# Moving four pieces of another stream's VectorE work inside a hand-ordered LSTM stage

## The chip, the cores and the metric

The kernel runs on one core of a Trainium2 chip. The metric is the device time of one execution in microseconds (us); each figure for a kernel is the median of several executions. The core has a matrix engine (TensorE, PE in the profile), a vector engine (VectorE, DVE), an activation engine (ScalarE, ACT), a general engine (GpSimd, POOL), and a sync engine (SyncE, SP) whose queue issues nearly all transfers here. Each engine takes its own instruction list, and semaphores tie the lists together.

## The reference

The input x is 128 graphs of 64 nodes with 256 channels, in f32. Four layers follow each other, each of the form x = x + layer(relu(layernorm(x))):

```
h = relu(layernorm(x)); x = x + gcn_with_batchnorm(h, adj, W1, W2)     # layer 0
h = relu(layernorm(x)); x = x + gcn_and_lstms(h, adj, Wg0, Wg1, ...)   # layer 1
h = relu(layernorm(x)); x = x + causal_attention(h, Wqkv, Wo)          # layer 2
h = relu(layernorm(x)); x = x + masked_attention(h, W, adj)            # layer 3
```

The change lies in layer 1. There h goes through two graph convolutions, relu(adj @ (h @ Wg)), and then through four LSTMs in a row. The LSTM number p (1 to 4) takes each graph's 64 nodes in windows of p nodes, runs p steps over a window from a zero state, and writes the last hidden state over the window's last node:

```
for p in 1..4:
    last = lstm(Wih[p-1], Whh[p-1], bias, windows of p nodes of h)
    h[:, p-1::p] = last
```

## The kernel before

The 8192 rows are cut into 16 chunks of 512 rows. Two chunks make a superchunk, so that layer 1 runs its LSTMs eight times, for superchunks 0 to 7. The LSTMs of one superchunk are a long chain of TensorE products and of gate work on the other engines. Between its links the kernel places work of other chunks by hand: the convolutions of the chunks of a later superchunk, and, for chunks whose LSTMs are done, the residual sum and the normalization that layer 2 needs. Nothing is scheduled by a planner: on TensorE, VectorE, ScalarE (from superchunk 0 on), GpSimd and SyncE, instructions are put into their queues in the order in which the program is written.

The program walks through the LSTMs with a generator, `lstms`, which yields at marked places. The marks have numbers: 0 to 3 in the one-token LSTM (`single`), 4 to 7 in the two-token one, 8 to 13 in the three-token one, 14 to 21 in the four-token one; a half (15.5, 19.5) is the place in the middle of a step. At each mark the loop runs the units that are listed for that number, one step of another generator each. The tuples that name the marks are the subject here:

- `CONV` and `FIRST` (the latter in superchunk 0) hold the marks for the next superchunk's two chunks in `convolutions`. `BEGUN` holds the marks for the first steps of the chunks after those. The first tuple of a pair is for the even chunk, the second for the odd one.
- The steps of `convolutions` are in order: scale (L900, two VectorE or ScalarE instructions into the tile `cv`); transpose (L988, two VectorE instructions into `ym`), after which SyncE writes `ym` to memory (L247), reads it back in another order into `cv` (L254) and loads the chunk's x into `xs` (L995); sum the two (`add_squares`, two instructions at L284); take the normalization's statistics (L159, L160, then two GpSimd instructions, L99 and L100); apply it in two halves (a small VectorE instruction L194, then two ScalarE instructions at L196 for each half); then products (`agg_b`, v, u, `agg_c`) and their evacuations.
- `AHEAD` and `FINAL` (the latter in superchunk 7) hold the marks of `ahead` for chunks whose layer 1 is done: write and reorder `xs`, statistics, two halves of the normalization, then `channel_squares` (four 32x32 block transposes by VectorE at L272, from `h` into `nm`), after which SyncE writes `nm` to memory for layer 2.

A step s of a p-token LSTM forms its gates from seven products each ("kinds") that share PSUM banks named x, y and z. VectorE adds a finished bank to the gates (L1164), and only then may TensorE put the next product into the same bank. ScalarE copies (L1161) and applies sigmoid and tanh (L1084); VectorE forms the cell (L1234, L1235) and the new state `hs` and its differences `hd` (L1093, L313 to L316), which the next step's products read. The first step of an LSTM is different: TensorE writes g (L1126), ScalarE applies the gate functions (L1113), VectorE forms the cell (L1119). At the end of superchunk's LSTMs VectorE forms the first operand sum `xd` of the next superchunk (L313), whose one-token LSTM starts with products at L1340, copies at L1360 and gate additions at L1364.

In superchunk 7 no convolutions are left, and short runs of transposes of an identity (`keep_busy`, L151) stand at some marks.

Of the kernel before, what the change touches and what calls it, by code (L numbers as in the profile page):

```python
# [19 lines left out]
def kernel(  # L20
# [1412 lines left out]
    def new_hT(sc):  # L1433

        hTs[sc] = l1r.tile([P, KD, SUP * CH], F32, tag="hT", name=f"hT_{sc}")
# [48 lines left out]

    RESIDUAL = (0, 3, 4), (2, 5, 5.5)
    CONV = (3, 4, 4, 5, 5.5, 7, 8, 9, 10, 10), (3, 4, 4, 11, 11.5, 13, 14, 15, 15.5, 17, 18, 20)
    BEGUN = (11, 11, 13, 14, 16), (17, 17.5, 19)
    FIRST = (1, 2, 3, 3, 4, 4, 5, 5.5, 7, 8, 9, 10, 10), (3, 3, 5.5, 7, 8, 8, 11, 11.5, 13, 14, 15, 15.5, 17, 18, 20)
    AHEAD = (4, 5, 7, 12, 14, 15), (6, 7)
    LATE = 5, 6, 8, 9  # L1490
    IDLE = {5: 4, 7: 18, 9: 10, 13: 14, 15: 8}
    FINAL = (4, 5, 10, 12, 12, 14), (6, 7, 11, 14, 14, 16)
    START = (0, 1, 0, 0, 0, 1, 0, 1, 1, 0, 0, 1, 1, 0, 1, 2, 2)

    tc.no_sync_barrier()
# [22 lines left out]
    with tc.manual_schedule(engines={mybir.EngineType.PE, mybir.EngineType.DVE, mybir.EngineType.Pool,  # L1518
                                     mybir.EngineType.Activation, mybir.EngineType.SP}):
        last = NCH // SUP - 1  # L1520
        for sc in range(last + 1):
            todo = {}

            def units(places, unit):
                for n in places:
                    todo.setdefault(n, []).append(unit)
# [4 lines left out]
            if sc < last:  # L1531
                for i in range(SUP):
                    units((CONV if sc else FIRST)[i], convs[(sc + 1) * SUP + i])
                new_hT(sc + 1)
# [7 lines left out]
            if sc:  # L1542
                for i in range(SUP):
                    units((FINAL if sc == last else AHEAD)[i], aheads[(sc - 1) * SUP + i])
            if sc + 1 < last:
                for i in range(SUP):
                    units(BEGUN[i], convs[(sc + 2) * SUP + i])
            n = -1
# [434 lines left out]
    def store(c, t):  # L1983
# [3 lines left out]
        for r in range(2):  # L1987
# [18 lines left out]

    FIRST = """table+0 load2+2 q2+0 copyq2+0 res1+14 res1+15 v2a+0 v2b+0 score2+0 res1+14 res1+15
               exp2+0 q2+1 divide2+0 copyq2+1 load2+3 turn2+0 v2a+1 v2b+1 out2+0 keep+0 res1+14 res1+15
# [10 lines left out]
    def run(order, c):  # L2019
        for name in order.split():  # L2020
            i = max(name.find("+"), name.find("-"))
            steps[name[:i]](c + int(name[i:]))

    with tc.manual_schedule(engines={mybir.EngineType.PE, mybir.EngineType.DVE,
                                     mybir.EngineType.Activation, mybir.EngineType.Pool,
                                     mybir.EngineType.SP}):
        run(FIRST, 0)
        close_l1r()
# [61 lines left out]
```

## Time and profile before

The time before is 1878.06 us, the median of 3 runs (1877.81 to 1878.57). The profiled execution spans 1877.4 us.

| what | profile before |
|---|---|
| TensorE busy | 1847.4 us, 98% |
| VectorE busy | 1245.6 us, 66% |
| ScalarE busy | 1014.0 us, 54% |
| GpSimd busy | 550.2 us, 29% |
| superchunks 0 to 7 of layer 1 | from about 276 us to 1506 us, 154.8 us each |
| sums, L284 of `convolutions`, one instruction | 0.69 us median |
| squares, L272, one instruction | 0.40 us median |
| statistics, L159, one instruction | 0.39 us median |
| VectorE's wait for the load of `xs` before L284 | 6.3 us in 6 times |

In a timeline, a line has the start, the time from the start to the end of the last instruction merged into it, the engine, the source line, the operation, the tiles (output<-input), the shape, the count, and in brackets the idle time of the engine before it and what ended it. Such times are from the start of the span. The end of a matmul is modelled, and matmuls overlap, so the step from one start to the next tells more of TensorE than its busy time: it is 0.11 us for 128 columns, 0.14 for 168, 0.22 for 256 and 0.43 for 512, and each f32 product is two MATMUL instructions.

### The profile page before, as it was taken

How to read it: one execution, taken by the hardware profiler on the slowest of the kernel's cores; microseconds unless marked ns; L12 is line 12 of the kernel's file. 1: busy time of each engine (PE TensorE's matmuls, PEld its weight loads, DVE VectorE, ACT ScalarE, POOL GpSimd, SP SyncE). 2: the span in 40 equal slices, each digit the busy share in tenths (PEclk: the TensorE clock that was granted, in tenths of full speed). 3: DMA queues.
4: the chain of work that ended last, by engine and by line, in shares of the span. 5: the costliest groups of instructions: out<-in, count | busy, mean ns of one | idle time of the engine just before them, and what ended most of it. 6: DMA issues, size and time to landing. Idle time of an engine off the chain costs nothing.

```text
span 1877.4 us, 39077 instructions
## 1 busy us (share of the span) xinstructions
PE 1847.4 (98%) x15077; PEld 1476.8 (79%) x15077; DVE 1245.6 (66%) x3150; ACT 1014.0 (54%) x2284; POOL 550.2 (29%) x704
## 2 busy tenths in 40 slices
PE   8999989999999999999999999999999999999998
PEld 6877856895897798699589689778968967777776
DVE  6768855566577666667666766666565567776776
ACT  5766635556456456555655645655565544444453
POOL 5855722122222212212322312222132114332232
PEclk9999999999999999999999999999999999999999
DMA  3223652134334433332433443343144254444433
GB/s 115 71 70 141 238 200 92 66 129 152 107 130 147 145 141 127 113 136 95 150 119 132 165 137 130 130 132 125 60 142 140 70 157 136 145 149 139 144 113 114
DMA packets 111273, 241.45 MB, mean 129 GB/s; under 512 B 11504, under 2 KB 74864, under 8 KB 111088
## 3 DMA queue, kind: packets, MB, share of 16 engines
q1 hardware_dynamic: 110192, 237.09, 37.6%
q8 instruction: 119, 1.95, 0.4%
q0 software_dynamic: 320, 1.05, 0.2%
q10 hardware_dynamic: 576, 0.82, 0.1%
q14 instruction: 66, 0.54, 0.1%
HBM read 170.50 MB, written 68.42 MB: 127 GB/s over the span
## 4 chain that ended last, share of the span: by engine, by line
PE 86%; DVE 6%; DMA 2%; ACT 2%; issue 1%; POOL 1%; SPq 0%; DVEq 0%; ACTq 0%
PE x L1155 20%; PE z L1155 10%; PE g L1126 9%; PE v L1580 5%; PE y L1155 5%; PE x L1340 4%; PE y L1340 3%; PE v L915 3%; PE u L929 3%; PE p_q L1587 3%; PE X L1776 3%; PE X L423 2%; PE X L499 2%; PE Y L1776 1%; PE Y L423 1%
## 5 line engine op out<-in xcount | busy, mean ns | idle before, releaser
L1155 PE MATMUL x<-xd,wset 128*128 128x128 f32 (+2 forms) x1152 | 256.9, 305 | 8.6 <-DVE gates L1164 8.4
L1155 PE MATMUL x<-hd,wset 128*128 128x128 f32 (+2 forms) x1152 | 255.3, 303 | 0.0
L1221 POOL TENSOR_TENSOR gates<-gates 128x512 f32<-128x512 f32 (+2 forms) x48 | 75.2, 1566 | 534.4 <-ACT gates L1084 534.4
L1084 ACT ACTIVATE gates<-gates,bias 128x256 f32<-128x256 f32 (+4 forms) x384 | 172.4, 488 | 103.7 <-DVE gates L1164 103.7
L1164 DVE TENSOR_TENSOR gates<-gates,x 128x128 f32<-128x128 f32 (+2 forms) x384 | 120.7, 321 | 144.8 <-PE x L1155 141.6
L1164 DVE TENSOR_TENSOR gates<-gates,z 128x128 f32<-128x128 f32 (+2 forms) x384 | 102.6, 319 | 150.3 <-PE z L1155 150.1
L1155 PEld LDWEIGHTS x<-xd,wset 128*128 128x128 f32 x1152 | 188.2, 192 | 16.6 <-DVE gates L1164 11.6
L1155 PEld LDWEIGHTS x<-hd,wset 128*128 128x128 f32 x1152 | 188.5, 192 | 5.0
L1126 PE MATMUL g<-hT,wset 128*128 128x256 f32 (+2 forms) x576 | 184.1, 474 | 0.1
L1126 PEld LDWEIGHTS g<-hT,wset 128*128 128x128 f32 x576 | 108.6, 190 | 68.1 <-issue 37.8
L1161 ACT COPY gates<-y 128x128 f32<-128x128 f32 (+2 forms) x192 | 53.9, 293 | 197.4 <-PE y L1155 195.6
L1155 PE MATMUL z<-hT,wset 128*128 128x128 f32 (+2 forms) x768 | 146.7, 303 | 0.0
L1155 PE MATMUL z<-hs,wset 128*128 128x128 f32 (+2 forms) x768 | 146.5, 303 | 0.2 <-DVE hs L1093 0.2
L1155 PEld LDWEIGHTS z<-hT,wset 128*128 128x128 f32 x768 | 117.3, 191 | 3.7
L1155 PEld LDWEIGHTS z<-hs,wset 128*128 128x128 f32 x768 | 117.2, 191 | 3.6 <-DVE hs L1093 0.3
L1113 ACT ACTIVATE gates<-g,bias 128x512 f32<-128x512 f32 (+2 forms) x144 | 74.9, 560 | 38.1 <-PE g L1126 37.5
L1084 ACT ACTIVATE gates<-x,bias 128x128 f32<-128x128 f32 (+2 forms) x192 | 75.0, 390 | 30.1 <-PE x L1155 27.7
L1155 PE MATMUL x<-hT,wset 128*128 128x128 f32 (+2 forms) x384 | 86.0, 306 | 0.2 <-ACT gates L1084 0.2
L1155 PE MATMUL x<-hs,wset 128*128 128x128 f32 (+2 forms) x384 | 84.9, 303 | 0.0
L1236 ACT ACTIVATE gates<-cell 128x256 f32<-128x256 f32 (+2 forms) x144 | 55.2, 383 | 48.4 <-DVE cell L1235 48.4
L1155 PE MATMUL y<-hd,wset 128*128 128x128 f32 (+2 forms) x384 | 79.7, 310 | 0.0
L1155 PE MATMUL y<-xd,wset 128*128 128x128 f32 (+2 forms) x384 | 77.5, 304 | 1.8 <-ACT gates L1113 1.8
(326 smaller groups left out, 4120.9 us busy)
## 6 DMA issues: line engine op xcount, KB each, us to landing
wset<-wfar SPq DMA_DIRECT2D x96, 960.0 KB, 6.5
hT<-far_h SPq DMA_DIRECT2D x124, 128.0 KB, 3.1
far_h<-hm SPq DMA_DIRECT2D x16, 512.0 KB, 2.8
far_n<-xs SPq DMA_DIRECT2D x16, 512.0 KB, 3.5
xs<-far_n SPq DMA_DIRECT2D x64, 128.0 KB, 4.6
far_x<-xs SPq DMA_DIRECT2D x16, 512.0 KB, 3.0
x<-far_x SPq DMA_DIRECT2D x64, 128.0 KB, 3.2
xt<-in_x_dram SPq DMA_DIRECT2D x15, 512.0 KB, 4.0
```

The costliest lines, as they stand in the source:

```text
L423: nc.tensor.matmul(self.banks[tag][:, i * CH // 2 : (i + 1) * CH // 2], w, self.at[kind], start=first and not i, stop=True, skip_group_che ...
L915: nc.tensor.matmul(banks[m], wg0_sb[:, k, m * P : (m + 1) * P], agg[:, k, :], start=(k == 0), stop=(k == KD - 1))
L929: nc.tensor.matmul(banks[j // 2][:, j % 2, :], v[:, k, j * P : (j + 1) * P], wg1_sb[:, k, :], start=(k == 0), stop=(k == KD - 1))
L1084: nc.scalar.activation(gate(q, c, part), src, AF.Tanh if q == 2 else AF.Sigmoid, bias=bs[:, q * KD + c : q * KD + c + 1])
L1113: nc.scalar.activation(columns_of(gate(q, c)), natural(banks[q, c][:, :n].rearrange("p (w b) -> p w b", b=nb)), AF.Tanh if q == 2 else AF. ...
L1126: nc.tensor.matmul(banks[q, c][:, :n].rearrange("p (w b) -> p w b", b=nb), wsets[p, q][:, 2 * k + c, :], hv[:, k, : (nw - 1) * p + 1 : p, ...
L1155: nc.tensor.matmul(folded(self.psum(kind)), wsets[p, self.q][:, BLOCKS[kind][i], :], (ox[self.s] if part == "x" else oh)[kind], start=firs ...
L1164: nc.vector.tensor_add(gate(self.q, *dst), gate(self.q, *a), self.psum(kind))
L1221: nc.gpsimd.tensor_mul(gates[:, 0, :, :n], gates[:, 0, :, :n], gates[:, 2, :, :n])
L1340: nc.tensor.matmul(folded(ps(g, kind)), wih1[:, g, KINDS1[kind], :], right[kind], start=kind in (2, 5, 1), stop=True, skip_group_check=True)
L1580: nc.tensor.matmul(ps[:, i, :], hT[:, k, j, :], w[:, k, first : first + D], start=(k == 0), stop=(k == KD - 1))
L1776: nc.tensor.matmul(st[c, tag][:, i * CH // 2 : (i + 1) * CH // 2].rearrange("p (a n) -> p a n", n=P), w, st[c, "o7"][kind], start=first an ...
```

## The change

Four tuples of marks change; the functions do not. The aim is to take other chunks' work off places where it stands ahead of the running LSTM's own instructions.

```diff
-    BEGUN = (11, 11, 13, 14, 16), (17, 17.5, 19)
-    FIRST = (1, 2, 3, 3, 4, 4, 5, 5.5, 7, 8, 9, 10, 10), (3, 3, 5.5, 7, 8, 8, 11, 11.5, 13, 14, 15, 15.5, 17, 18, 20)
-    AHEAD = (4, 5, 7, 12, 14, 15), (6, 7)
+    BEGUN = (11, 11, 13, 14, 16), (17, 17.5, 21)
+    FIRST = (1, 2, 3, 3, 4, 4, 5, 5.5, 7, 8, 9, 10, 10), (1, 2, 4, 5, 6, 8, 11, 11.5, 13, 14, 15, 15.5, 17, 18, 20)
+    AHEAD = (4, 5, 7, 12, 14, 19), (6, 7)
...
-    FINAL = (4, 5, 10, 12, 12, 14), (6, 7, 11, 14, 14, 16)
+    FINAL = (4, 5, 9.5, 10, 12, 13), (6, 7, 11.5, 14, 14, 15)
```

Read by unit:

- In superchunks 0 to 5 the sums of the odd chunk of two superchunks later go from mark 19 (before the last step of the four-token LSTM) to mark 21 (its end).
- In superchunks 1 to 6 the squares of the even chunk of the superchunk before go from mark 15 to mark 19.
- In superchunk 0, for chunk 3: scaling 3 to 1, transposes 3 to 2, sums 5.5 to 4, statistics 7 to 5, the first half of the normalization 8 to 6; its second half stays at 8.
- In superchunk 7, for chunk 12: statistics 10 to 9.5, first half of the normalization 12 to 10, squares 14 to 13; for chunk 13: statistics 11 to 11.5, squares 16 to 15.

The built programs have the same order of instructions on TensorE. On VectorE, ScalarE, GpSimd and SyncE only the named pieces move; the squares of chunk 12 keep their place in VectorE's order, since nothing of VectorE lies between marks 13 and 14. In SyncE's queue the write of `nm` comes behind the transfers of mark 17.5 where it came ahead of them.

## The prediction

> **What bounds the kernel now.** I read the page first, then the timelines of TensorE and VectorE around each edited place, then the timelines of ScalarE there, and one table of stretches.
>
> ```profile
> PE 1847.4 (98%) x15077; PEld 1476.8 (79%) x15077; DVE 1245.6 (66%) x3150; ACT 1014.0 (54%) x2284; POOL 550.2 (29%) x704
> PE 86%; DVE 6%; DMA 2%; ACT 2%; issue 1%; POOL 1%; SPq 0%; DVEq 0%; ACTq 0%
> ```
>
> TensorE is the bound nearly everywhere, and the change leaves its instructions in the same order. So it can only win what TensorE stands still for, a few microseconds. Where it stands still in superchunk 3 at mark 19:
>
> ```profile
> 884.91 0.29 DVE L316 TENSOR_TENSOR hd<-hs,hd 128x128 f32<-128x128 f32 x1
> 886.49 1.29 DVE L284 TENSOR_TENSOR xs<-xs,cv 128x512 f32<-128x512 f32 x2 [1.29 <-DMA xs<-in_x_dram]
> 887.70 0.48 DVE L1164 TENSOR_TENSOR gates<-gates,x 128x128 f32<-128x128 f32 x2
> ...
> 886.59 0.39 PE L1155 MATMUL y<-hd,wset 128*128 128x128 f32 x2
> 888.03 0.49 PE L1155 MATMUL x<-xd,wset 128*128 128x128 f32 x2 [1.06 <-DVE gates L1164]
> ```
>
> Two sums (L284) stand in VectorE's queue ahead of the gate additions (L1164). They wait 1.29 us for the load of xs, take 1.21, and TensorE must wait for the first addition, because its next x product goes into the bank being read. Its regular step is 0.11 per MATMUL, so it lost 888.03 - 886.59 - 0.22 = 1.22. The same subtraction at this place gives, for superchunks 0 to 5: 0.86, 0.38, 1.34, 1.23, 0.18, 2.00; 6.0 us in sum. Superchunk 6 has no sums there, and shows the room:
>
> ```profile
> 1350.13 0.29 DVE L316 TENSOR_TENSOR hd<-hs,hd 128x128 f32<-128x128 f32 x1
> 1351.40 0.29 DVE L1164 TENSOR_TENSOR gates<-gates,x 128x128 f32<-128x128 f32 x1 [0.98 <-PE x L1155]
> ```
>
> After the longest of these stops TensorE ran at half clock for a while (third number from the end: the granted clock):
>
> ```profile
> 1193.00:1195.00 2.00, 2.00 (x21) 2.00 (x19) 0.62 (x3) 0.49 (x3) 0.00 (x0) 1.00 0.74 245
> 1197.30:1201.30 4.00, 3.97 (x21) 3.97 (x22) 1.45 (x7) 1.54 (x4) 0.00 (x0) 0.57 0.00 0
> ```
>
> The first superchunk stops once before the three-token LSTM, where four ScalarE normalizations wait for VectorE's statistics and stand ahead of the first gate activations. The last stops behind statistics at mark 10 and squares at mark 16:
>
> ```profile
> 342.05 2.07 ACT L196 ACTIVATE cv<-xs,nmr_b,rstd_b 128x256 f32<-128x256 f32 x4 [4.59 <-DVE nmr_b L194]
> 344.69 0.89 PE L1155 MATMUL y<-xd,wset 128*128 128x168 f32 x4 [1.11 <-ACT gates L1113]
> ...
> 1434.27 0.57 DVE L1164 TENSOR_TENSOR gates<-gates,z 128x168 f32<-128x168 f32 x2 [3.73 <-PE z L1155]
> 1438.31 0.55 PE L1155 MATMUL x<-xd,wset 128*128 128x168 f32 x2 [1.30 <-DVE gates L1164]
> 1478.33 0.49 PE L1155 MATMUL x<-xd,wset 128*128 128x128 f32 x2 [0.74 <-DVE gates L1164]
> ```
>
> **What the Trainium skill says.** Perfetto Trace Analysis, section Tensor Engine Instruction: VectorE, ScalarE and GpSimd take their instructions strictly in order. The trace agrees: ready gate additions stood behind the waiting sums for 1.29 us. TensorE: Matmul & The Clock Gate, section What's actually happening: the clock is halved after an idle window of about 3.4 us that runs freely. The trace has one such stretch, 3.4 us from 1197.9, after a stop of 2.00; stops up to 1.46 drew none. SBUF — State Buffer, section Who interferes with whom: VectorE and GpSimd share a port pair under an exclusive lock. The scaling at L900 took 0.54 with GpSimd idle and 1.03 beside it.
>
> **The change part by part.** Times below are TensorE's.
>
> *Mark 19, superchunks 0 to 6.* The sums leave. In 1 to 6 the four squares (L272) come from mark 15: 855.33 to 856.67 in superchunk 3, 1.34 us to the next start, and without a DMA wait, since their input was normalized long before. They would start 0.20 after L316, so L1164 comes at 1350.13 + 0.20 + 1.34 = 1351.67, and TensorE may go on 0.33 later (888.03 - 887.70), at 1352.00; in superchunk 6 it went on at 1352.02. So they fit, by a hair: cost 0 to 0.3 each, I take 0. Saved: 6.0, and 0.1 after each of six stops, where the next pair takes 0.33 and not 0.22: 6.6. The half clock costs 3.4/2 = 1.7; its window runs freely, so I count it in the range only.
>
> *Mark 15.* The squares leave a place where VectorE idles 2.50 us before L1164 at 859.25 and TensorE loses nothing: 0.
>
> *Mark 21.* The sums come between L313 and L1364: 898.47 + 0.60 + 1.21 = 900.28, against 900.12 now, where L1364 waits for ScalarE's copies. The first product that needs these additions is at 903.46. Their load has landed 12 us before. What queues behind (additions, residual transposes, L1356 with 1.19 idle) takes 0.16 later: 0.
>
> *First superchunk, gain.* Statistics go from mark 7 to 5, where VectorE idles 8.09 before 317.06, and two of four normalizations to mark 6, into ScalarE's 1.81 idle. At mark 8 only two remain, ready early. The stop of 1.27 (y at 344.69) goes, with 0.1 after it: 1.4. The sums go from 5.5 to 4, where they wait for their load: the transposes that feed the round trip through memory will end near 297.0 (294.89, where L1350 follows the statistics today, + 0.94 + 1.20 from below), and from there to the landing it took 8.7 to 10.5 us in the six superchunks (876.77 to 886.49 in superchunk 3), so the sums start at 305.7 to 307.5 and end 1.21 later. Behind them stand the cells (L1119), which without them would come at 303.93 + 1.9: a delay of up to 2.9. The hd that follows from them is ready at 307.04 today, 4.6 us before TensorE's y<-hd at 311.61: hidden, with 1.7 to spare.
>
> *First superchunk, cost.* Two scalings (2 x 0.47, GpSimd idle) now stand at mark 1 and two transposes (1.20) at mark 2, all ahead of the second stream's scale nmr_b, on a VectorE with gaps of at most 0.17:
>
> ```profile
> 297.81 2.08 ACT L196 ACTIVATE cv<-xs,nmr_b,rstd_b 128x256 f32<-128x256 f32 x4 [1.59 <-DVE nmr_b L194]
> 298.50 0.77 PEld L214 LDWEIGHTS agg_b<-adjt_bd,cv 64*64 64x64 f32 x32 [0.76 <-ACT cv L196]
> ```
>
> TensorE already follows these normalizations tile by tile, so what delays them delays it: 0.94 + 1.20 - 0.2 of gaps absorbed = 1.9. If the stop draws a half-clock window, 1.7 more.
>
> *Last superchunk.* Statistics of 2.13 us (1435.83 to 1437.96) go from mark 10 to 9.5, into the 3.73 idle before 1434.27; two normalizations fit ScalarE's 4.36 idle before 1438.29. The stop at 1438.31 (1438.31 - 1436.71 - 0.14 = 1.46) goes. The other statistics go from 11 to 11.5, into 3.73 idle before 1452.49: a stop of 0.27 goes. The squares go from 16 to 15, into 1.91 idle before 1470.54: a stop of 0.91 goes, and the chain behind them, which stops TensorE for 0.36 and 0.31 more at 1482 and 1484, starts 0.4 earlier against it. With 0.1 after three stops: 1.46 + 0.27 + 0.91 + 0.3 + 0.4 = 3.3. Stops at 1458 and 1464 (0.24, 0.90) stay: the squares at mark 13 keep their place in VectorE's order, ahead of the same normalizations.
>
> Sum: 6.6 + 1.4 + 3.3 - 1.9 = 9.4; 1878.06 - 9.4 = 1868.7 us.
>
> **The rivals.** (a) All as above: 1868.7. With the old half clock also in the timed runs, 1867.0. (b) Mixed: squares at mark 19 cost 0.3 in each of six superchunks (1.8), and the first superchunk draws a half-clock window (1.7): 1872.2. For it speaks the margin of 0.02 us; against it that stops up to 1.46 drew no window. (c) No change: the gain at mark 19 is taken back by a wait later in the same superchunk, and the half-clock window comes: 1878.06 - 1.4 - 3.3 + 1.9 + 1.7 = 1877.0. Against it: superchunk 6 runs that stage without the stop and shows none behind it. (d) Slower: squares and sums lie bare at the new places, 6 x 1.34 + 6 x 1.21 = 15.3: 1868.7 + 15.3 = 1884.0. For it speaks only that VectorE is 66% busy; against it the slack of 1.2 and 3.3 us just read.
>
> **How the numbers follow.** (a) 0.60, (b) 0.29, (c) 0.08, (d) 0.03. The time is that of (a), 1868.7. The range goes from 1865.8, (a) with 1.7 of clock and a smaller first-superchunk cost, 1867.0 - 1.2, to 1873.2, (b) with a sum wait of 1.0 that I hid. Bound for faster is 1878.06 - 3.76 = 1874.3: faster takes (a), (b): 0.89; same 0.08; slower 0.03.
>
> **What would show it.** Right: the wait on xs's load at L284 gone at mark 19 and L1164 within 0.3 of the time it has in superchunk 6; no PE idle at the places of 344.69, 1438.31 and 1478.33; agg_b of the second stream some 1.9 later. Wrong: PE waiting for L1364 or for L1340's banks after a boundary, L1119 in the first superchunk holding up y<-hd, or a second half-clock stretch.

## The result and the profile after

| kernel | median us | range | runs |
|---|---|---|---|
| before | 1877.93 | 1877.37 to 1878.57 | 4 |
| after | 1867.99 | 1867.58 to 1868.96 | 4 |

The ratio is 0.9948, with a 95% interval of 0.9930 to 0.9965: faster by 9.9 us, where 9.4 was predicted. The profiled span is 1866.5 us.

From the page of the changed kernel, the busy times:

```profile
PE 1844.3 (99%) x15077; PEld 1476.6 (79%) x15077; DVE 1251.4 (67%) x3150; ACT 1013.4 (54%) x2284; POOL 554.1 (30%) x704
```

TensorE has the same 15077 instructions and is busy for 3.1 us less, but the span is 10.9 us shorter: what went is mostly time in which TensorE stood. VectorE has the same instructions and is busy for 5.8 us longer, so some of them became slower at their new places; where, is seen below.

The length of each superchunk (from its first L1340 product to the next one's, and for the last to the first product of layer 2, L1587), worked out from the starts in the traces, says where the time went:

| kernel | 0 | 1 | 2 | 3 | 4 | 5 | 6 | 7 |
|---|---|---|---|---|---|---|---|---|
| before | 158.22 | 153.94 | 154.90 | 154.79 | 153.74 | 157.19 | 152.96 | 146.44 |
| after | 157.24 | 153.52 | 153.52 | 153.52 | 153.52 | 153.67 | 153.02 | 143.18 |

In the kernel before no two of superchunks 1 to 5 were alike; now they are alike to 0.15 us. The unequal part was a wait for transfers, as the experiments show. (The 154.8 us of the table ahead of the prediction is superchunk 3's length; the eight are not alike.)

The timelines of VectorE and TensorE at mark 19 of superchunk 3, after:

```profile
882.63 0.29 DVE L316 TENSOR_TENSOR hd<-hs,hd 128x128 f32<-128x128 f32 x1
882.84 1.42 DVE L272 STREAM_TRANSPOSE nm<-h 128x256 f32<-128x256 f32 x4
884.18 0.46 DVE L1164 TENSOR_TENSOR gates<-gates,x 128x128 f32<-128x128 f32 x2
...
884.30 0.39 PE L1155 MATMUL y<-hd,wset 128*128 128x128 f32 x2
884.52 0.45 PE L1155 MATMUL x<-xd,wset 128*128 128x128 f32 x2
```

The sums are gone and the squares take their place, for 1.34 us to the next start. TensorE's step from y<-hd to x<-xd is 884.52 - 884.30 = 0.22, its regular one, where it was 1.44 before.

The same at mark 21, with GpSimd; the first two lines are of the kernel before:

```profile
900.12 1.28 DVE L1364 TENSOR_TENSOR gates<-gates,x 128x512 f32<-128x512 f32 x2 [0.97 <-ACT gates L1360]
899.43 1.27 POOL L314 TENSOR_TENSOR xd<-hT 128x512 f32<-128x512 f32 x1
...
894.92 0.69 DVE L313 TENSOR_TENSOR xd<-hT 128x512 f32<-128x512 f32 x1
895.52 2.63 DVE L284 TENSOR_TENSOR xs<-xs,cv 128x512 f32<-128x512 f32 x2
898.07 1.27 DVE L1364 TENSOR_TENSOR gates<-gates,x 128x512 f32<-128x512 f32 x2
...
895.22 0.70 POOL L1099 TENSOR_TENSOR hT<-gates 128x128 f32<-128x128 f32 x1 [5.80 <-ACT gates L1236]
895.88 1.72 POOL L314 TENSOR_TENSOR xd<-hT 128x512 f32<-128x512 f32 x1
...
897.33 2.74 PE L1340 MATMUL y<-xd,wih 128*128 128x512 f32 x6
899.90 2.74 PE L1340 MATMUL x<-xd,wih 128*128 128x512 f32 x6
```

Two sums take 2.55 us here (898.07 - 895.52) instead of 1.21, while GpSimd works beside them; that GpSimd is the reason is borne out by all traces, in the last section. Still, the additions behind them end their first pair at 899.34, and TensorE's next x product starts in its regular step, 2.57 after the one ahead of it.

The first superchunk, after, at the second stream's normalizations and at the sums; the first line is of the kernel before:

```profile
297.08 0.69 DVE L194 SCALAR_TENSOR_TENSOR nmr_b<-mv_b,rstd_b 128x4 f32<-128x4 f32 x1
...
296.32 1.27 DVE L988 STREAM_TRANSPOSE ym<-cv 128x512 f32<-128x512 f32 x2
...
299.83 0.15 DVE L194 SCALAR_TENSOR_TENSOR nmr_b<-mv_b,rstd_b 128x4 f32<-128x4 f32 x1
...
307.15 1.29 DVE L284 TENSOR_TENSOR xs<-xs,cv 128x512 f32<-128x512 f32 x2 [3.14 <-DMA xs<-in_x_dram]
308.37 1.29 DVE L1119 TENSOR_TENSOR cell<-gates 128x512 f32<-128x512 f32 x2
...
294.13 5.31 PE L1126 MATMUL g<-hT,wset 128*128 128x512 f32 x12
300.67 1.94 PE L214 MATMUL agg_b<-adjt_bd,cv 64*64 64x64 f32 x64 [1.22 <-ACT cv L196]
302.54 5.42 PE L1126 MATMUL g<-hT,wset 128*128 128x512 f32 x12
```

The transposes stand ahead of the normalization's first instruction, and TensorE now stops for 1.38 us ahead of agg_b. The sums wait 3.14 us, longer than any wait at mark 19, but the hd behind them is there in time.

The last superchunk, after, at the two places where TensorE stood for 1.46 and 0.91:

```profile
1427.04 0.57 DVE L1164 TENSOR_TENSOR gates<-gates,z 128x168 f32<-128x168 f32 x2 [1.60 <-PE z L1155]
...
1429.05 0.73 PE L1155 MATMUL y<-xd,wset 128*128 128x168 f32 x4
1429.62 0.45 PE L1155 MATMUL x<-xd,wset 128*128 128x168 f32 x2
...
1467.72 0.61 PE L1155 MATMUL y<-xd,wset 128*128 128x128 f32 x4
1468.17 0.39 PE L1155 MATMUL x<-xd,wset 128*128 128x128 f32 x2
```

VectorE's idle time before the z additions fell from 3.73 to 1.60: the statistics filled it. TensorE goes from y to x in the regular time of four products (0.57 and 0.45) at both places.

### The profile page after: what moved, and what is told of

It reads as the page before. It is cut to its first block, busy times and chain, and to the rows that moved or that the text cites. A ratio compares the mean times of both kernels' runs of the same rounds, so it can differ in the third digit from the quotient of the medians.

```text
span 1866.5 us, 39078 instructions
## 1 busy us (share of the span) xinstructions
PE 1844.3 (99%) x15077; PEld 1476.6 (79%) x15077; DVE 1251.4 (67%) x3150; ACT 1013.4 (54%) x2284; POOL 554.1 (30%) x704
## 4 chain that ended last, share of the span: by engine, by line
PE 90%; DVE 5%; ACT 2%; issue 1%; POOL 1%; DMA 1%; SPq 0%; DVEq 0%; ACTq 0%; POOLq 0%
PE x L1155 22%; PE z L1155 11%; PE g L1126 9%; PE y L1155 6%; PE v L1580 5%; PE x L1340 4%; PE y L1340 3%; PE u L929 3%; PE v L915 3%; PE p_q L1587 3%; PE X L1776 3%; PE X L423 2%; PE X L499 2%; PE Y L423 1%; PE Y L1776 1%
## 5 line engine op out<-in xcount | busy, mean ns | idle before, releaser
L1221 POOL TENSOR_TENSOR gates<-gates 128x512 f32<-128x512 f32 (+2 forms) x48 | 75.1, 1565 | 497.1 <-ACT gates L1084 497.1
L1164 DVE TENSOR_TENSOR gates<-gates,x 128x128 f32<-128x128 f32 (+2 forms) x384 | 120.9, 321 | 149.5 <-PE x L1155 146.5
L1164 DVE TENSOR_TENSOR gates<-gates,z 128x128 f32<-128x128 f32 (+2 forms) x384 | 102.4, 318 | 146.2 <-PE z L1155 146.2
L1595 POOL TENSOR_TENSOR s<-s,mx 128x256 f32<-128x256 f32 (+2 forms) x33 | 40.4, 1225 | 128.1 <-DVE mx L1594 120.3
```

Of the source, the lines that this page charges most:

```text
L1164: nc.vector.tensor_add(gate(self.q, *dst), gate(self.q, *a), self.psum(kind))
L1221: nc.gpsimd.tensor_mul(gates[:, 0, :, :n], gates[:, 0, :, :n], gates[:, 2, :, :n])
```

## The experiments

Where a kernel follows a variant of the tuples, only the edited tuple is shown. The kernel before was timed again beside each group, and ratios are against those runs. Stops of TensorE are steps from start to start less the regular step; the first steps behind a stop are some 0.1 us longer too.

**Each of the four edits alone.** First the sums, the squares untouched:

```diff
-    BEGUN = (11, 11, 13, 14, 16), (17, 17.5, 19)
+    BEGUN = (11, 11, 13, 14, 16), (17, 17.5, 21)
```

> The kernel before with one edit: the sums of the odd chunk (L284) go from mark 19 to mark 21. Theory: TensorE's stops at mark 19 came from these sums and their wait for the load alone, and mark 21 has room, so all of it shows here: 6.0 us of stops and 0.6 after them, 1877.9 - 6.6 = 1871.3; no PE idle before the x product after the last y<-hd of mark 19 in any superchunk. Rival 1, the sums lie bare at mark 21: 1871.3 + 6 x 1.2 = 1878.5, with L1364 late by over 1 us. Rival 2, the squares' leaving mark 15 carries part of the gain: clearly less than 6 us here.

Measured: 1870.51 us against 1878.63, ratio 0.9959 (0.9947 to 0.9972), 8.1 us by the medians: more than the 6.6 expected, which leaves out the half clock. Superchunks 1 to 5 take 153.44 to 153.46, and the half-clock stretch is gone. This edit is most of the gain. In the changed kernel, with the squares at mark 19 as well, superchunks 1 to 4 take 153.52 and 5 takes 153.67: the squares cost 0.08 each in 1 to 4. Of the 0.22 in superchunk 5 only 0.07 stand at mark 19; the rest is a stop at 1182.3, ahead of that mark, which a kernel shown below has too (the first of the two that combine what helped, 153.11 where the second takes 152.95) although its squares stand at mark 15. So it isn't the squares' doing; what it is stays open.

The squares at mark 19 while the sums stay there:

```diff
-    AHEAD = (4, 5, 7, 12, 14, 15), (6, 7)
+    AHEAD = (4, 5, 7, 12, 14, 19), (6, 7)
```

> The kernel before with one edit: the squares of the even chunk (L272) go from mark 15 to mark 19, where the sums stay, behind them. Theory: VectorE is idle while the sums wait for their load, so the squares (1.34 us) fill that wait and delay the sums only by what exceeds it. With waits before of 0.44, 1.40, 1.29, 0.23 and 2.06 us in superchunks 1 to 5: 0.9 + 0 + 0.05 + 1.1 + 0 = 2.1 us slower, 1880.0. Rival 1, squares at mark 19 cost their length wherever they stand: 6 x 1.34 = 8.0 slower, 1885.9. Rival 2, mark 15 was a loss that the profile hid: faster than before.

Measured: 1880.12 us, ratio 1.0007 (0.9998 to 1.0015), so the time alone doesn't tell it from no change; 2.1 us slower was expected. The trace does. VectorE at mark 19 of superchunk 1:

```profile
577.41 1.42 DVE L272 STREAM_TRANSPOSE nm<-h 128x256 f32<-128x256 f32 x4
578.75 1.25 DVE L284 TENSOR_TENSOR xs<-xs,cv 128x512 f32<-128x512 f32 x2
579.92 0.48 DVE L1164 TENSOR_TENSOR gates<-gates,x 128x128 f32<-128x128 f32 x2
```

The squares run where VectorE would have waited for the load, and the sums follow them bare. The stops of superchunks 1 to 5 are 1.17, 2.10, 1.15, 1.17 and 1.51, 7.1 in sum, where they were 5.1: the 2.1 expected. The trace has no half-clock stretch at this mark, and where runs of the kernel before have one, that takes back up to 1.7. The place holds one of the two pieces, and not both.

The first superchunk alone, and the last one alone:

```diff
-    FIRST = (...), (3, 3, 5.5, 7, 8, 8, 11, ...)
+    FIRST = (...), (1, 2, 4, 5, 6, 8, 11, ...)
...
-    FINAL = (4, 5, 10, 12, 12, 14), (6, 7, 11, 14, 14, 16)
+    FINAL = (4, 5, 9.5, 10, 12, 13), (6, 7, 11.5, 14, 14, 15)
```

> The kernel before with one edit: the first superchunk's places of chunk 3 (scaling 1, transposes 2, sums 4, statistics 5, first half of the normalization 6). Theory: the stop of 1.4 us before the three-token LSTM goes, and agg_b of chunk 2 starts 1.7 to 1.9 us later against the LSTM: net 0.3 to 0.5 slower, about 1878.3. Rival, only the gain counts and the delay at agg_b is taken back later in the superchunk: 1876.5.

> The kernel before with one edit: the last superchunk's places (statistics of chunk 12 at 9.5, its normalization at 10 and 12, squares at 13; statistics of chunk 13 at 11.5, squares at 15). Theory: stops of 1.46, 0.27 and 0.91 us and 0.3 after them go, and at most 0.4 of the chain behind: 2.9 to 3.3 faster, 1874.8. Rival, the gain is lost again before the end of the stage at the stops before and in the four-token LSTM: 1877.0 or more.

Measured: FIRST 1878.68 us, ratio 1.0001 (0.9993 to 1.0009); FINAL 1874.86 us, ratio 0.9982 (0.9976 to 0.9989), 3.4 us. The edit of the first superchunk shows no gain: it exchanges a stop of 1.27 and what follows it for one of 1.39 and a smaller one ahead of it, and its superchunk takes 158.26 for 158.22.

**Is it the place or the wait?** The gain at mark 19 could come from taking 1.21 us of sums off the place, or only from no longer waiting there. Here the sums stay, and their data comes earlier:

```diff
-    BEGUN = (11, 11, 13, 14, 16), (17, 17.5, 19)
+    BEGUN = (11, 11, 13, 14, 16), (17, 17, 19)
```

> The kernel before with BEGUN odd (17, 17, 19): the sums stay at mark 19, but the transposes come at mark 17 directly behind the scaling, so that the round trip through memory starts about 2.3 us earlier. Theory (it is the wait for the data that cost time at mark 19, not the 1.21 us of the sums): L284 waits for nothing, its 1.21 fits where squares of 1.34 fitted, and the six stops at mark 19 (6.0, with the half clock behind the last of them 7.7) go. At mark 17, 0.94 of scaling and 1.20 of transposes stand ahead of the gate additions where 1.34 fit: a new stop of 0.8 and 0.1 after it in each of six superchunks, 5.4. Net -1.2 to -2.9 in time; in the trace no stop at mark 19. Rival (the place costs, whoever waits): 0.4 to 1.2 stay in each of the six stops at mark 19, and the new stops come on top: +1 to +5.

Measured: 1876.18 us against 1878.73, ratio 0.9985 (0.9979 to 0.9992), 2.6 us faster. VectorE at marks 17 and 19 of superchunk 3:

```profile
872.22 1.00 DVE L900 TENSOR_SCALAR cv<-z1a,sc_bn,sh_bn 128x512 f32<-128x512 f32 x2
873.25 1.31 DVE L988 STREAM_TRANSPOSE ym<-cv 128x512 f32<-128x512 f32 x2
874.48 0.45 DVE L1164 TENSOR_TENSOR gates<-gates,x 128x128 f32<-128x128 f32 x2
...
885.63 0.29 DVE L316 TENSOR_TENSOR hd<-hs,hd 128x128 f32<-128x128 f32 x1
885.93 1.29 DVE L284 TENSOR_TENSOR xs<-xs,cv 128x512 f32<-128x512 f32 x2
887.14 0.48 DVE L1164 TENSOR_TENSOR gates<-gates,x 128x128 f32<-128x128 f32 x2
```

L284 stands where it stood, waits for nothing, and TensorE has no stop over 0.15 there in any of the six superchunks. The wait cost the time, not the 1.21 us of the sums, which fit when nothing is waited for. At mark 17 the transposes leave too little room, and a stop of 0.66 to 0.67 comes in each superchunk; it was expected at 0.8. These take back 4.6 of the gain (six of 0.67 and 0.1 behind it).

**Could the wait have been shortened where it is?** In the kernel before, the load of xs is issued behind the four reads and lands last:

```diff
-        get(dst, far)
         xs[c] = res.tile([P, NJ, D], F32, tag=f"r{c}", name=f"xs_{c}")
         nc.sync.dma_start(xs[c], xr[c])
+        get(dst, far)
```

> The kernel before, with the load of xs issued ahead of the four reads instead of behind them; the sums stay at mark 19. Theory: the wait of L284 is for the last of five transfers in SyncE's queue, and only the reads have to follow the write of ym. With the load out of the way the last read lands up to 1.75 us earlier (the estimate: what lay between the landing of the last read and of the load in the kernel before). Four of the six stops at mark 19 (0.86, 0.38, 1.23, 0.18) go, and 1.34 and 2.00 shrink to 0.3 or less: with the half clock behind the 2.00, about -6, near 1872.5 us. Rival: the five transfers share the same DMA engines, so the last of them lands when it did and the name of the load in the wait is only that of the last to come: no change, 1878.6, with L284 waiting for a read of cv in place of xs.

Measured: 1879.42 us against 1876.78, ratio 1.0014 (1.0007 to 1.0020): slightly slower, where 6 us faster was expected. The theory fell. SyncE's queue in the kernel before, superchunk 3:

```profile
876.79 0.32 SPq L247 DMA_DIRECT2D far_y<-ym  x1
879.55 1.74 SPq L254 DMA_DIRECT2D cv<-far_y  x4
881.34 0.43 SPq L995 DMA_DIRECT2D xs<-in_x_dram  x1
```

and in the variant, with VectorE's wait:

```profile
877.43 0.32 SPq L247 DMA_DIRECT2D far_y<-ym  x1
880.07 0.38 SPq L994 DMA_DIRECT2D xs<-in_x_dram  x1
880.56 1.87 SPq L254 DMA_DIRECT2D cv<-far_y  x4
...
887.26 1.29 DVE L284 TENSOR_TENSOR xs<-xs,cv 128x512 f32<-128x512 f32 x2 [1.42 <-DMA cv<-far_y]
```

The load goes out first now, but no earlier than 2.64 us behind the write: xs has the tag of ym in a pool of one buffer for each tag, so it may be filled only when the write has read ym. The last of the five transfers, now a read, lands no earlier than before: the sums start 9.83 us behind the write (887.26 - 877.43), and 9.70 in the kernel before (886.49 - 876.79). Over the six superchunks it is 9.2 to 10.1 us, and 8.6 to 10.5 before; the six waits sum to 7.4 us where they summed to 6.3. This is what the rival said would be seen, but its reason isn't shown: the fifth transfer is issued as late as before too, and this kernel doesn't separate the shared DMA engines from the times of issue. A buffer of its own for xs wasn't tried.

**The first superchunk, done otherwise.** Scaling and transposes go back to mark 3, behind the second stream's normalization; sums and statistics share mark 5.5:

```diff
-    FIRST = (...), (1, 2, 4, 5, 6, 8, 11, ...)
+    FIRST = (...), (3, 3, 5.5, 5.5, 6, 8, 11, ...)
```

> The changed kernel with other places of chunk 3 in the first superchunk: scaling and transposes back at mark 3, sums and statistics both at mark 5.5, first half of the normalization at 6 as in the change. Theory: the delay of agg_b (1.7 us in the trace) comes from the scaling and transposes ahead of nmr_b alone, and VectorE's idle 3.29 us at mark 5.5 holds the statistics: agg_b follows g without the stop, the stop before the three-token LSTM stays away, 1.7 us faster than the changed kernel. Rival, the delay comes from the statistics chain of chunk 2 itself: no faster.

Measured: 1867.88 us, where the changed kernel, run again in the same session, took 1868.12 (1867.71 to 1868.42): no gain in the time, where 1.7 was expected. (The five runs of the changed kernel lie within 0.7 us, the nine of the kernel before in that session within 4.0; with the wait gone from TensorE's way, its changing length is gone too.) The stop at agg_b went, but another came at mark 6, of 0.81. GpSimd, VectorE and TensorE there:

```profile
327.49 2.35 POOL L1221 TENSOR_TENSOR gates<-gates 128x1024 f32<-128x1024 f32 x1
...
327.79 2.07 DVE L194 SCALAR_TENSOR_TENSOR nmr_b<-mv_b,rstd_b 128x4 f32<-128x4 f32 x1
329.78 0.74 DVE L1164 TENSOR_TENSOR gates<-gates,x 128x256 f32<-128x256 f32 x2
...
330.25 0.70 PE L1155 MATMUL x<-xd,wset 128*128 128x256 f32 x2 [0.65 <-DVE gates L1164]
```

An instruction on four elements a partition, 0.15 us elsewhere, took 2.07 and ended when GpSimd's ended (329.86 and 329.84). So the next kernel puts both halves of the normalization at mark 8:

```diff
-    FIRST = (...), (3, 3, 5.5, 5.5, 6, 8, 11, ...)
+    FIRST = (...), (3, 3, 5.5, 5.5, 8, 8, 11, ...)
```

> The changed kernel with FIRST of the odd chunk (3, 3, 5.5, 5.5, 8, 8, 11, ...): scaling and transposes behind the second stream's normalization, sums and statistics both at mark 5.5, both normalization halves at mark 8, so that no small L194 stands beside GpSimd's L1221 at mark 6. Theory (port lock): L194 takes 0.15 again, the stop of 0.81 at mark 6 goes, and superchunk 0 takes 156.46 - 0.81 = 155.6: -1.6 against the changed kernel, about 1866.5. Rival: four normalizations at mark 8 again stand ahead of the first gate activations, and the stop of 1.27 before the three-token LSTM comes back, since statistics at 5.5 are early but ScalarE has 2.08 us more in front of L1113: then -0.3 to -0.5, about 1867.7.

Measured: 1865.92 us (1865.71 to 1866.42), and superchunk 0 takes 155.53 us, 1.71 less than in the changed kernel and 0.93 less than in the kernel just shown. The gain is read from the traces; against the kernel before, the ratio is 0.9943 (0.9930 to 0.9955), and the changed kernel's 0.9946 (0.9934 to 0.9958) in another session can't be told from it. VectorE, ScalarE and TensorE at mark 8:

```profile
339.09 0.15 DVE L194 SCALAR_TENSOR_TENSOR nmr_b<-mv_b,rstd_b 128x4 f32<-128x4 f32 x1
...
339.28 2.07 ACT L196 ACTIVATE cv<-xs,nmr_b,rstd_b 128x256 f32<-128x256 f32 x4 [1.76 <-DMA wset<-wfar]
341.26 1.83 ACT L1113 ACTIVATE gates<-g,bias 128x336 f32<-128x336 f32 x4
...
336.70 6.94 PE L1126 MATMUL g<-hT,wset 128*128 128x336 f32 x24
343.48 0.73 PE L1155 MATMUL y<-xd,wset 128*128 128x168 f32 x4
```

Four normalizations stand again ahead of the gate activations, as before the change, but they start at once, and y follows the g products without a stop. What stopped TensorE there in the kernel before was statistics that came late, not normalizations that were too many.

**Beyond the change.** One stop of 0.40 us is left in each of superchunks 0 to 5, where two normalizations (mark 16) stand ahead of the gate activations:

```diff
-    BEGUN = (11, 11, 13, 14, 16), (17, 17.5, 21)
+    BEGUN = (11, 11, 13, 14, 15.5), (17, 17.5, 21)
```

> The changed kernel with one more edit: the first half of the even chunk's normalization (L194, two at L196) goes from mark 16 to 15.5. Theory: the stop of 0.40 us that stays in superchunks 0 to 5 in the first step of the four-token LSTM comes from ScalarE's two normalizations ahead of the gate activations; ScalarE has 1.67 us idle before them: 6 x 0.5 = 3.0 us faster than the changed kernel. Rival, at 15.5 they hold up ScalarE's copies out of the x banks, and TensorE waits there instead: the same or slower.

Measured: 1865.48 us (1865.31 to 1866.17), 2.6 less than the changed kernel in the same session; against the kernel before the ratio is 0.9933 (0.9920 to 0.9945). Superchunks 1 to 4 take 153.02, 0.50 less each.

All that helped, together, first with the FIRST that gained nothing in the time, then with the better one, which the edit shows:

```diff
-    BEGUN = (11, 11, 13, 14, 16), (17, 17.5, 21)
-    FIRST = (...), (1, 2, 4, 5, 6, 8, 11, ...)
-    AHEAD = (4, 5, 7, 12, 14, 19), (6, 7)
-    FINAL = (4, 5, 9.5, 10, 12, 13), (6, 7, 11.5, 14, 14, 15)
+    BEGUN = (11, 11, 13, 14, 15.5), (17, 17.5, 21)
+    FIRST = (...), (3, 3, 5.5, 5.5, 8, 8, 11, ...)
+    AHEAD = (4, 5, 7, 12, 14, 15), (6, 7)
+    FINAL = (4, 5, 9.5, 10, 12, 13), (6, 7, 11.5, 12, 14, 15)
```

> The changed kernel with the edits of the two kernels before this one, and two more: the first half of chunk 13's normalization in the last superchunk at 12 and not 14, and the squares in superchunks 1 to 6 back at mark 15. Theory: 1.7 and 3.0 us as there; the stop of 0.90 us before the four-token LSTM of the last superchunk goes (1.0); the squares at mark 19 cost 0.08 us in each of six superchunks (0.5): 6.2 us faster than the changed kernel. Rival, gains that share VectorE and ScalarE do not add: 3 us or less.

> The combination of before (BEGUN even at 15.5, squares back at 15, FINAL odd statistics at 12) with this FIRST of (3, 3, 5.5, 5.5, 8, 8, ...) in place of (3, 3, 5.5, 5.5, 6, 8, ...). Theory: superchunk 0 loses its 0.81 stop and nothing else moves: 1863.1 - 0.8 = 1862.3. Rival: the stop before the three-token LSTM comes back at 1.27: 1863.6.

Measured: 1863.10 us (1862.35 to 1863.42), then 1861.30 us (1860.90 to 1862.10); both ratios are 0.9919 (0.9905 to 0.9932), since the kernel before took 1876.78 in the second session and 1878.65 in the first. Against the changed kernel the first is 5.0 us faster, where 6.2 was expected. The traces separate the two: superchunk 0 takes 155.95 in the first and 155.03 in the second, and 1 to 6 take 152.95 in both, but for superchunk 5 of the first. Superchunk 7 takes 142.0: a stop of 0.90 went with the first half of chunk 13's normalization at mark 12, and one of 0.28 came, again from a small L194 beside GpSimd. VectorE and GpSimd of the second kernel:

```profile
1437.96 0.94 DVE L194 SCALAR_TENSOR_TENSOR nmr_n<-mv_n,rstd_n 128x4 f32<-128x4 f32 x1
...
1437.27 1.61 POOL L1221 TENSOR_TENSOR gates<-gates 128x672 f32<-128x672 f32 x1
```

Both are faster than both kernels of the case, by about 15 us against the kernel before.

## Why the prediction held, step by step

**Mark 19.** Predicted 6.6, and 1.7 of half clock in the range alone. In the traces superchunk 0 lost 0.96 of its length at this mark (its stop of 0.86 and 0.1 behind it), superchunks 1 to 5 lost 6.81 together, and superchunk 6 took 0.06 longer: 7.7, of which 1.7 is the half clock of superchunk 5. That leaves 6.0. Of the 0.6 short of 6.6, 0.46 are the squares, taken at 0: against the kernel with the sums moved alone they cost four times 0.08, and 0.07 each in superchunks 5 and 6. The other 0.15 is the stop in superchunk 5 that isn't theirs. L1164 stands 1.55 behind L316 (884.18 - 882.63); the limit read in superchunk 6 of the kernel before was 1352.02 - 0.33 - 1350.13 = 1.56, so "by a hair" was right.

**Mark 15.** 0 as predicted: through superchunk 3, the starts of TensorE's products shift against those of the kernel before at mark 19 (1.23) and nowhere else by over 0.06.

**Mark 21.** Predicted L1364 0.16 later, and nothing for TensorE. TensorE lost nothing, but the size was wrong. From the first L1340 product, L1364 starts 5.89 after (898.07 - 892.18), and it started 4.40 after in the kernel before: 1.49 later. The term mis-sized is the 1.21 of the sums, taken from a place where GpSimd idles; at this place they take 2.55. Nor was all of the 3.3 us slack that the prediction read from L1364's start to the product at 903.46: the first pair of additions takes 1.28 of it. The Trainium skill has it on the page SBUF — State Buffer, section Who interferes with whom, which the prediction cited but applied only to L900. That TensorE lost nothing with a delay nine times the predicted one was luck: the first pair of additions now ends 899.90 - 899.34 = 0.56 us ahead of that product.

**First superchunk, gain.** Predicted 1.4; the stop of 1.27 is gone, as predicted, but with it went 0.4 behind it and not 0.1: TensorE's products win back 1.66 between 344.69 and 346.13. The delay of the cells didn't stop y<-hd either, and the wait for the load ended at 307.15, inside the predicted 305.7 to 307.5.

**First superchunk, cost.** Predicted 1.9. The g products behind agg_b start 28.15 after the superchunk's first product (302.54 less its start at 274.39), and 26.46 in the kernel before (300.33 - 273.87): 1.69. L194 starts 2.23 later by the same measure, but takes 0.15 where it took 0.69 beside GpSimd, and so ends 1.69 later; those 0.54 are the term left out. Also left out is a second place: the scalings at mark 1 stand ahead of gate additions (L1364), and 0.35 of the 1.69 arises there: TensorE's next x product (L1340) starts at 291.48, right behind the first x addition's end at 291.33, where in the kernel before it didn't wait. No half-clock stretch came in this superchunk. Gain and cost cancel, as the kernel with FIRST alone shows; a loss of 0.5 was predicted.

**Last superchunk.** Predicted 3.3: 1.46, 0.27 and 0.91 for three stops, 0.3 behind them, 0.4 for the chain. All three stops are gone, and those of 0.24 and 0.90 stayed, as predicted. Superchunk 7 takes 146.44 - 143.18 = 3.26 less. By the starts of TensorE's products, the three stops and what is behind them give 3.1. The chain gives nothing and not 0.4: its two stops of 0.36 and 0.31 became 0.04, 0.19 and 0.39. The last 0.16 is a stop at 1501.5 that the changed kernel lacks and the kernel with FINAL alone still has, so this edit didn't remove it. That the sum is met is in part luck.

**The sum.** Predicted 9.4, timed 9.9. From the superchunks of the two traces it is 7.7 + 0.0 + 3.3 = 11.0, with the half-clock stretch of the kernel before, and 9.3 without it; the 0.6 missing at mark 19 and the 0.5 not lost in the first superchunk nearly cancel, which is luck too. The timed difference lies between the two. The mean clock of each run tells how common such stretches are, though not where they fall: of 99 timed runs of the kernel before in the four groups of experiments, 30 have 0.998 or less, which takes at least one whole stretch (each lowers the mean over 1878 us by 0.0009), and 29 have 1.000, which leaves room for none. Within each group the median of the former is 1.6 to 2.5 us longer. The changed kernel isn't free of them: its two traces have one each outside superchunks 0 to 7, from 33.45 and from 253.23. Rival (b), with the squares at 0.3 each and a half clock in the first superchunk, fell on both; (c) fell since nothing was taken back in the same superchunk; (d) fell with the regular steps at both new places.

## What to carry to other kernels

A small piece of work put ahead of a critical instruction on the same engine costs nothing while the engine has slack, but its wait is passed on whole: ask first when its data lands, and then how long it runs. Before moving it, look at what GpSimd does at the new place: beside GpSimd the sums, the scaling and even the four-element L194 took longer, while transposes and statistics did not. Of two ways to give it time, a later use and an earlier start, take the one whose place has idle time left: here the later use cost nothing, and the earlier start paid most of the gain back.

## What the hardware showed that was not expected

The length of a tiny VectorE instruction depends on its neighbour: L194 on 128x4 elements took 0.15 us with GpSimd idle, 0.94 beside an L1221 of 1.61 us, and 2.07 beside one of 2.35. Both long ones ended within 0.02 of GpSimd's instruction. The fourteen traces hold 392 of them: 360 take 0.15 to 0.16, and each of the 32 that ran wholly beside a GpSimd instruction takes 0.23 to 2.07 and ends within 0.03 of its end. At mark 21 the two L284 took 0.95 and 1.76 beside L1099 and L314, for 0.69 elsewhere, and GpSimd's own L314 took 1.72 there, for 1.27 in the kernel before. Over all traces, L284 of `convolutions` takes 0.65 to 0.69 where GpSimd is idle (128 times) and 0.77 to 1.76 where GpSimd works during at least nine tenths of it (186 times). Not every instruction is so: the squares, L272, take 0.39 to 0.45 with GpSimd idle (798 times) and 0.40 to 0.44 beside it (756 times), and the statistics, L159, 0.39 to 0.43 both ways. This agrees with the lock that the Trainium skill describes (SBUF — State Buffer, section Who interferes with whom); that an instruction of 0.15 us becomes fourteen times longer is what the traces add.

A stop of some 2 us halved the clock in three traces and not in a fourth. In the kernel before, the one with FIRST alone and the one with FINAL alone, a half-clock stretch follows the stop of superchunk 5 at mark 19 (2.00, 2.05 and, of 2.49 in all, 2.19 ahead of the stretch). The stretches last 3.41 us, and the starts of two in one trace are a whole number of windows apart (253.71 and 1199.20 in the kernel with FINAL alone: 945.49 = 277 x 3.4133). The stretch of the kernel before starts at 1197.88, so the 3.41 us ahead of it, from 1194.47, held the whole stop of 2.00. In the kernel with the squares alone a stop of 2.10, at 733.8 to 735.9, drew none: by the grid of its own stretch at 253.97 a boundary fell at 735.25 and cut the stop into 1.45 and 0.65. This agrees with the free-running window on the skill's page TensorE: Matmul & The Clock Gate, section What's actually happening. The window needn't be idle throughout, as 2.00 of 3.41 us were enough. How much is enough isn't shown: stretches ahead of layer 1, as that at 253.71, follow windows in which TensorE stood for less (1.35 us there, by the modelled ends of its instructions). The price at mark 19 is 1.7 us, and whether the same stop pays it depends, in these four traces, on where it falls.
